# Regrouping the stages of the block chains that lead from the second layer's last product into the third layer

## The chip, the cores and the metric

The kernel runs on one core of a Trainium2 chip. The metric is device time in microseconds (us). One execution taken by the profiler gives the page and the trace that are read here; the median of five timed runs stands beside it.

## The reference, cut to what matters

A graph network of four layers works on x (4096 nodes, 128 features) and one adjacency matrix adj (4096 x 4096, about 0.2% non-zero, kept dense, float32). Each layer is `x = layernorm(x + layer(x, adj))`:

```python
x = _layernorm(x + _L0_gnn_ref(x, adj, adj, ...))   # signed attention
x = _layernorm(x + _L1_gnn_ref(x, adj, ...))        # Chebyshev, K = 3, two convolutions, elu after each
x = _layernorm(x + _L2_gnn_ref(x, adj, ...))        # attention, 4 heads of 32 features
x = _layernorm(x + _L3_gnn_ref(x, adj, ...))        # mean over neighbours
```

The second layer (`_L1_gnn_ref`) ends with a product of adj with a 4096 x 128 matrix, an elu and the layer norm. The third (`_L2_gnn_ref`) is, for every head: `tau = adj_t * exp(max(0.2 C, C))` with `C = alpha_src + alpha_dst`, a sum `tau_sum` over the sources, and `z = sum(adj_t * tau / tau_sum * h_prime)`, where `h_prime = x @ weight.T`.

## The kernel before, in words

The nodes lie in 8 blocks of 512 (`NB = 8`, `IB = 512`), each of 4 tiles of 128. This text calls the last product of the second layer the *big product*; its eight blocks of targets are the loop over `ib` (line L1118). Each block takes 32 matmuls of a 128 x 128 stationary tile against 512 columns. A float32 matmul is recorded as two instructions, so that a block shows 64 of them; a transposition is recorded once.

Three kinds of work are laced into that loop by hand, in an order that PE, DVE, ACT and POOL keep as it is written (`tc.manual_schedule`); the DMA issues on SP are not part of it.

*Block chains.* When block `ib` of the big product is complete, its chain finishes the layer for these 512 nodes. `block_end(ib)` is a generator; each `yield` ends a stage. Its stages, with names that this text uses:

- **elu** (L749 to L753): DVE adds the product, DVE and ACT make the elu in `oT`. It is written at once at the block's end. L749 also frees bank `pp`, in which the next block of the big product accumulates.
- **T1** (L757): four transpositions of `oT` on PE into `px`.
- **N** (L759 to L769): DVE adds to x and takes the statistics, ACT the root, DVE the reciprocal, ACT four activations that normalise x.
- **T2** (L771): four transpositions of x into `px`.
- **C** (L773 to L775): ACT copies to `xT` and loads the table of Exp, POOL adds a bias to x.
- **H0, h0, H1, h1**: H (L784) is two products with `W2S` into `px`, one for each half of the block; h (L791 to L795) reads them, ACT with two exponentials and DVE with two multiplications into `hc`.

`block_targets(ib)` follows with **D** (L804, a product into `px`), **E** (L806, L807: ACT, an exponential and a copy) and **S** (L809 to L813: the split of the result in three bfloat16 parts, which goes DVE, ACT, ACT, DVE, ACT). The last of S on ACT is the last reader of `px`. The pool `ps_x` has one buffer, one PSUM bank: T1, T2, H0, H1 and D of all blocks go through the one `px`, and each waits until the one before it has been read.

*The queue.* The chains stand in one deque, `chains`, and `one(chains)` takes one stage of the first of them; where a generator ends within a call, the call goes on to the next chain. In blocks 3 to 7 of the big product it is called twice in each group of `cuts`: after the group's first half and at its end. With one chunk in a group that is after every 2 matmuls, with two chunks after every 4. A *slot* m is the call after matmul m of the 32. Block 3 has the slots 4, 8, 12, ... 32; blocks 4 and 5 have 2, 4, 6, 8, 12, 16, 18, 20, 22, 24, 28, 32; blocks 6 and 7 have 4, 8, 12, 16, 18, 20, 22, 24, 28, 32.

*Steps of the third layer.* In blocks 3 to 7 each group also carries one source tile `nt` of the third layer for two passes, p0 and p1 (two pairs of heads for the first 1024 targets). ACT copies the tile of adj into the one PSUM buffer `a` (L852); for p0 and then p1 DVE makes `tau` (L880, twice) and a part of `tau2` (L886), and POOL the rest of `tau2` (L887, L888). Every group ends with four products on PE, `num` and `den` (L904, 8 recorded instructions each). The order of a group is: copy `a`, step p0, first half of the matmuls, slot, step p1, second half, slot, four products. Tile `nt` may be started only when the chain of the block that holds it has passed its last stage (`ended`).

The stages of `block_end` are parted by yields such as these, and the halves of H by this loop:

```python
yield
if ib <= 2:
    yield
...
if ib < NB - 2:
    yield
for half in range(2):
```

Of the kernel before, what the change touches and what calls it, by code (L numbers as in the profile page):

```python
# [33 lines left out]
def adj_resnorm_d4(ctx: ExitStack, tc: tile.TileContext, x_in, xT_in, adj, adjT, w0g, w0gT, a0, w1a, b1a,  # L34
# [10 lines left out]
    NB = N // IB  # L45
# [87 lines left out]
    def transpose4(pool, name, src, order=lambda r: r):  # L133

        p = pool.tile([P, TB, P], F32, name=name)
        for k in range(TB):
            order(nc.tensor.transpose(p[:, k, :], src(k), ident))  # L137
        return p

    def stats(r, t):  # L140
        st = small.tile([P, 6], F32, name="st")
        nc.vector.bn_stats(st, r)
        nc.vector.bn_aggr(mv[:, t, :], st)
# [481 lines left out]
    def network(usual):  # L625

        with ExitStack() as whole:
# [113 lines left out]
            def block_end(ib, p):  # L741

                blk = slice(ib * IB, (ib + 1) * IB)
                tb = slice(ib * TB, (ib + 1) * TB)
                pns = []
                oT = l2w.tile([P, IB], F32, name="oT", tag="z")
                rn = l2w.tile([P, 2, IB], F32, name="rn", tag="nd")
                r, n = rn[:, 0, :], rn[:, 1, :]
                nc.vector.tensor_add(oT, p, h0T[:, blk])  # L749
                nc.vector.tensor_scalar(n, oT, B1B, 0.0, op0=ALU.add, op1=ALU.min)  # L750
                nc.scalar.activation(n, n, AF.Exp)
                nc.scalar.activation(r, oT, AF.Relu, bias=B1B)
                nc.vector.scalar_tensor_tensor(oT, n, -1.0, r, op0=ALU.add, op1=ALU.add)  # L753
                yield
                if ib <= 2:
                    yield
                q = transpose4(ps_x, "px", lambda k: oT[:, k * P:(k + 1) * P])  # L757
                yield
                nc.vector.tensor_add(x[:, tb, :], q, x[:, tb, :])  # L759
                for t in range(ib * TB, (ib + 1) * TB):  # L760
                    stats(x[:, t, :], t)
                s = small.tile([P, TB], F32, name="rstd")
                m = small.tile([P, TB], F32, name="mean")
                nc.scalar.activation(s, mv[:, tb, 1], AF.Sqrt, bias=eps)
                nc.vector.reciprocal(s, s)
                nc.vector.scalar_tensor_tensor(m, mv[:, tb, 0], -1.0, s, op0=ALU.mult, op1=ALU.mult)
                for k in range(TB):
                    r = x[:, ib * TB + k, :]
                    nc.scalar.activation(r, r, AF.Identity, bias=m[:, k:k + 1], scale=s[:, k:k + 1])  # L769
                yield  # L770
                q = transpose4(ps_x, "px", lambda k: x[:, ib * TB + k, :])  # L771
                yield
                nc.scalar.copy(xT[:, blk], q.rearrange("p k i -> p (k i)"))  # L773
                nc.scalar.activation(m[:, 0:1], m[:, 0:1], AF.Exp, scale=0.0)
                nc.gpsimd.tensor_tensor(x[:, tb, :], x[:, tb, :], B2R[:, None, :].to_broadcast([P, TB, F]), ALU.add)  # L775
                if ib < NB - 2:
                    yield
                for half in range(2):

                    pool, name = (ps_p, "pp") if ib == NB - 1 and half else (ps_x, "px")  # L780
                    pn = pool.tile([P, 2, F + H], F32, name=name)
                    for k in range(2):
                        t = ib * TB + 2 * half + k
                        nc.tensor.matmul(pn[:, k, :], xT[:, t * P:(t + 1) * P], W2S, start=True, stop=True)  # L784
                    pns.append(pn)
                    if ib == NB - 1 and half == 0:
                        continue
                    yield
                    for pn, at in zip(pns, range(half + 1 - len(pns), half + 1)):
                        two = slice(ib * TB + 2 * at, ib * TB + 2 * at + 2)  # L790
                        nc.scalar.activation(cs[:, two, :], pn[:, :, F:F + H], AF.Exp, scale=0.2)  # L791
                        nc.scalar.activation(es[:, two, :], pn[:, :, F:F + H], AF.Exp, scale=0.8)
                        for k in range(2):
                            t = ib * TB + 2 * at + k
                            nc.vector.tensor_mul(hc[:, t], pn[:, k, 0:F].rearrange("p (h f) -> p h f", f=FO),  # L795
                                                 cs[:, t, :][:, :, None].to_broadcast([P, H, FO]))
                    pns.clear()
                ended.append(ib)

            def block_targets(ib):  # L800

                blk = slice(ib * IB, (ib + 1) * IB)
                pd = ps_x.tile([96, IB], F32, name="px")
                nc.tensor.matmul(pd, WD, xT[:, blk], start=True, stop=True)  # L804
                yield
                nc.scalar.activation(pd, pd, AF.Exp, scale=-0.8)  # L806
                nc.scalar.copy(dv[:, blk], pd)  # L807
                yield
                nc.vector.tensor_sub(pd, pd, dv[:, blk])  # L809
                nc.scalar.copy(dv[32:64, blk], pd[32:64, :])  # L810
                nc.scalar.copy(dv[64:96, blk], pd[64:96, :])
                nc.vector.tensor_sub(pd[64:96, :], pd[64:96, :], dv[64:96, blk])
                nc.scalar.copy(dv[64:96, blk], pd[64:96, :])  # L813
                if ib < 2:
                    yield
# [220 lines left out]
            with tc.manual_schedule(engines={mybir.EngineType.PE, mybir.EngineType.DVE, mybir.EngineType.Activation,  # L1036
# [40 lines left out]
                def num(this, nt, tau2):  # L1077
                    this.product(False, nt, tau2)
                    if nt == NT - 1 and this is not passes[-1]:
                        if this is passes[0]:  # L1080
                            first_sums.close()
                            ps_a.append(enter(name="ps_a2", bufs=1, space=PSUM))
                        chains.append(this.finish())
                        if this.heads[-1] == H - 1:
                            chains.append(layer3_blocks(this.blocks))
                            chains.append(start_product(this.blocks))
                            if this is passes[1]:
                                chains.append(block_targets(NB - 1))
                        later = passes.index(this) + 2
                        if 2 < later < len(passes):  # L1090
                            chains.append(passes[later].targets())
# [13 lines left out]
                for ib in range(NB):  # L1105
                    early = ib == 1
                    p = ps_nd.tile([P, IB], F32, name="num") if early else ps_p.tile([P, IB], F32, name="pp")
                    cuts = [0, 2, 4, 6, 8] if ib < 4 else [0, 1, 2, 4, 5, 6, 8] if ib < 6 else [0, 2, 4, 5, 6, 8]
                    for first, last in zip(cuts, cuts[1:]):
                        ks = [(c, k) for c in range(first, last) for k in range(TB)]  # L1110
                        for n, (c, k) in enumerate(ks):
                            if ib > 2 and n in (0, len(ks) // 2):
                                if n == 0:
                                    load()
                                step()
                            if k == 0:
                                a = chunk(ld, adjT, ib, c)
                            nc.tensor.matmul(p, w[:, c * TB + k, :], a[:, k, :], start=c == 0 and k == 0,  # L1118
                                             stop=c == NB - 1 and k == TB - 1)
                            if n + 1 in (len(ks) // 2, len(ks)) or ib <= 2 and k % 2:  # L1120
                                one(chains)
                        if last == NB:
                            end = block_end(ib, p)
                            next(end)
                            chains.append(end)
                            if ib < NB - 1:
                                chains.append(block_targets(ib))
                            if ib < 2:
                                chains += [this.targets(range(ib, 4, 2)) for this in passes[0:2]]
                        if ib > 2:  # L1130
                            products()
# [79 lines left out]
```

## Time and profile before

| what | value |
|---|---|
| median of 5 runs | 2223.66 us (2220.61 to 2225.76) |
| the profiled execution, its own time | 2222.86 us |
| its span in the trace | 2221.0 us |
| PE busy | 2134.7 us, 96% of the span |
| DVE busy | 1186.5 us, 53% |
| POOL busy | 857.7 us, 39% |
| ACT busy | 562.8 us, 25% |
| DMA | 528.18 MB, mean 238 GB/s |

The span is the time between the first and the last recorded instruction; 1.86 us of the execution's own time lie outside it. The blocks of the big product can be told in the trace by L749, which starts as each block's last matmul is done: it starts at 1169.55 us for block 2, 1211.39 for block 3, 1272.49 for block 4, 1329.81 for block 5, 1380.51 for block 6 and 1430.55 for block 7. "In block 4" below means the stretch in which the big product's block 4 runs, which is when the chain of block 3 is worked off.

### The profile page before, as it was taken

Reading aid. Unit: us, or ns where it says so; the run is one execution under the profiler, and the core shown is the slowest. Engines: PE = TensorE matmul, PEld = TensorE weight load, DVE = VectorE, ACT = ScalarE, POOL = GpSimd, SP = SyncE. Lnnn points to the kernel's source line nnn. Section 1 sums busy time; section 2 is a strip of 40 time slices with the busy share of each in tenths; the row PEclk is TensorE's granted clock in tenths of the full one; section 3 lists DMA queues with packets and bytes.
Section 4 is the critical chain, followed back from the end, with each engine's and each line's share of the span. In section 5 each row is a group of like instructions: output and inputs, shape, how many; then the busy total and the mean of one; then the engine's idle time right before and its main releaser. Section 6 shows DMA issues by size and latency. Waiting matters only on the chain. (4 is left out here: it accounts for less than half of the span.)

```text
span 2221.0 us, 22997 instructions
## 1 busy us (share of the span) xinstructions
PE 2134.7 (96%) x8640; PEld 847.9 (38%) x8644; DVE 1186.5 (53%) x1832; ACT 562.8 (25%) x1014; POOL 857.7 (39%) x539
## 2 busy tenths in 40 slices
PE   8999999999999999999999999979999899999997
PEld 3444454444444444444443333322222222223333
DVE  5655560000011110000017777799999999999995
ACT  6755010000000000000032323335333433232213
POOL 0000000000000000000005676698999899989980
PEclk9999999999999999999999999999999999999999
DMA  9886658888767667777876556525666566635554
GB/s 395 337 326 234 223 192 290 300 301 303 265 229 260 240 233 269 263 264 264 292 256 232 189 195 218 209 82 193 240 231 241 190 244 230 228 133 191 189 174 170
DMA packets 87145, 528.18 MB, mean 238 GB/s; under 512 B 9328, under 2 KB 15472, under 8 KB 25712
## 3 DMA queue, kind: packets, MB, share of 16 engines
q1 hardware_dynamic: 80288, 521.64, 66.8%
q10 hardware_dynamic: 6736, 4.98, 0.7%
q8 instruction: 70, 1.15, 0.2%
q14 instruction: 51, 0.42, 0.1%
HBM read 524.49 MB, written 2.10 MB: 237 GB/s over the span
## 5 line engine op out<-in xcount | busy, mean ns | idle before, releaser
L880 DVE SCALAR_TENSOR_TENSOR tau<-D,es,a 128x1024 f32<-128x1024 f32 (+1 forms) x640 | 646.7, 1059 | 45.9 <-ACT a L852 20.0
L888 POOL TENSOR_TENSOR tau<-tau,chunk 128x1024 f32<-128x1024 f32 x192 | 459.6, 2394 | 13.3 <-DVE tau L880 12.7
L775 POOL TENSOR_TENSOR x<-x,B2R 128x512 f32<-128x512 f32 x8 | 10.2, 1276 | 1143.8 <-PE px L137 1143.8
L904 PE MATMUL num<-tau,hc 128*32 128x512 f32 x2048 | 331.6, 614 | 15.6 <-POOL tau L888 9.1
L904 PE MATMUL den<-tau,cs 128*32 128x512 f32 x2048 | 337.5, 603 | 1.8 <-DVE tau L880 0.4
L991 PE MATMUL pp<-chunk,xT 128*128 128x512 f32 (+1 forms) x488 | 231.7, 604 | 0.0
L852 ACT ACTIVATE a<-chunk 128x1024 f32<-128x1024 f32 x160 | 164.4, 1027 | 248.7 <-DVE tau L886 188.1
L664 PE MATMUL pacc<-chunk,t 128*128 128x512 f32 x512 | 223.5, 592 | 0.0
L664 PE MATMUL pacc<-chunk,v 128*128 128x512 f32 x512 | 222.5, 592 | 0.0
L664 PE MATMUL pacc<-chunk,x 128*128 128x512 f32 x512 | 222.1, 592 | 0.0
L887 POOL TENSOR_TENSOR tau<-tau,chunk 128x320 f32<-128x320 f32 x192 | 168.2, 876 | 128.0 <-DVE tau L880 85.3
L1118 PE MATMUL pp<-chunk,w 128*128 128x512 f32 x448 | 203.1, 598 | 0.8 <-DVE oT L749 0.8
L379 PE MATMUL pacc<-chunk,hw 128*128 128x512 f32 x408 | 188.2, 606 | 0.8 <-DVE hw L421 0.7
L886 DVE TENSOR_TENSOR tau<-tau,a 128x704 f32<-128x704 f32 x186 | 163.4, 878 | 0.0
L894 POOL TENSOR_TENSOR tau<-tau,chunk 128x1024 f32<-128x1024 f32 x64 | 151.7, 2371 | 1.1
L904 PEld LDWEIGHTS num<-tau,hc 128*32 128x32 f32 x2048 | 61.3, 110 | 229.8 <-issue 129.2
L904 PEld LDWEIGHTS den<-tau,cs 128*32 128x32 f32 x2048 | 79.0, 111 | 174.6 <-issue 99.0
L664 PEld LDWEIGHTS pacc<-chunk,v 128*128 128x128 f32 x512 | 97.2, 190 | 122.0 <-issue 122.0
L664 PEld LDWEIGHTS pacc<-chunk,x 128*128 128x128 f32 x512 | 96.3, 190 | 115.8 <-issue 115.8
L664 PEld LDWEIGHTS pacc<-chunk,t 128*128 128x128 f32 x512 | 96.1, 190 | 115.3 <-issue 115.3
L991 PEld LDWEIGHTS pp<-chunk,xT 128*128 128x128 f32 x488 | 85.7, 189 | 128.6 <-issue 125.8
L711 DVE COPY w<-ptr 128x512 f32<-128x512 f32 x8 | 5.5, 692 | 241.5 <-PE ptr L137 241.5
(243 smaller groups left out, 1687.8 us busy)
## 6 DMA issues: line engine op xcount, KB each, us to landing
chunk<-in_adjT SPq DMA_DIRECT2D x386, 1024.0 KB, 4.8
chunk<-in_adj SPq DMA_DIRECT2D x80, 1024.0 KB, 4.9
chunk<-in_adj SPq DMA_DIRECT2D x32, 512.0 KB, 4.7
keep<-in_adjT SPq DMA_DIRECT2D x13, 1024.0 KB, 9.9
xT<-in_xT ACTq DMA_DIRECT2D x8, 256.0 KB, 6.7
out<-o ACTq DMA_DIRECT2D x7, 256.0 KB, 2.3
W1A<-in_w1a ACTq DMA_DIRECT2D x1, 384.0 KB, 5.6
W1B<-in_w1b ACTq DMA_DIRECT2D x1, 384.0 KB, 7.6
```

The lines of the kernel that those rows point to most:

```text
L379: in_order(nc.tensor.matmul(p, hw[:, j * TB + k, :], a[:, k, :], start=first and k == 0, stop=last and k == TB - 1))
L664: nc.tensor.matmul(p, stationary(c * TB + k), a[:, k, :], start=n == 0 and k == 0, stop=n == NB - 1 and k == TB - 1)
L775: nc.gpsimd.tensor_tensor(x[:, tb, :], x[:, tb, :], B2R[:, None, :].to_broadcast([P, TB, F]), ALU.add)
L852: nc.scalar.activation(ap, a, AF.Copy, accum_out=deg[:, nt, self.mp:self.mp + 1])
L880: nc.vector.scalar_tensor_tensor(flat(tau[:, q:q + n]), flat(self.D[:, q:q + n]), es[:, nt, head:head + 1], ap, op0=ALU.max, op1=ALU.mult)
L886: nc.vector.tensor_tensor(t2[:, 0:OWN], t[:, 0:OWN], (a if only else ap)[:, 0:OWN], ALU.mult)
L887: nc.gpsimd.tensor_tensor(t2[:, OWN:WB], t[:, OWN:WB], a[:, OWN:WB], ALU.mult)
L888: nc.gpsimd.tensor_tensor(t2[:, WB:2 * WB], t[:, WB:2 * WB], a, ALU.mult)
L894: nc.gpsimd.tensor_tensor(tau2[:, 2:4, :], tau[:, 2:4, :], rep(a, 2), ALU.mult)
L904: nc.tensor.matmul(acc[32 * q:32 * q + 32, :], weights(nt, head, is_den), r[:, q, :], start=nt == 0, stop=nt == NT - 1)
L991: nc.tensor.matmul(p, y[:, c * TB + k, :], a[:, k, lo:lo + n], start=c == blocks[0] and k == 0, stop=end)
L1118: nc.tensor.matmul(p, w[:, c * TB + k, :], a[:, k, :], start=c == 0 and k == 0, stop=c == NB - 1 and k == TB - 1)
```

## The change

Four yields move. In `block_end`, block 2 loses the empty stage ahead of T1 (blocks 0 and 1 keep it) and the yield between C and H0. Blocks 3 and 4 get a yield ahead of H1, so that h0 and H1 are no longer taken in one call. In `block_targets`, blocks 3 to 6 get a yield ahead of D, so that h1 and D are no longer taken in one call. No instruction is added or taken away; the places of the stages among the matmuls and steps change.

```diff
-                if ib <= 2:
+                if ib < 2:
                     yield
                 q = transpose4(ps_x, "px", lambda k: oT[:, k * P:(k + 1) * P])
...
-                if ib < NB - 2:
+                if ib < NB - 2 and ib != 2:
                     yield
                 for half in range(2):
 
                     pool, name = (ps_p, "pp") if ib == NB - 1 and half else (ps_x, "px")
+                    if half and ib in (3, 4):
+                        yield
                     pn = pool.tile([P, 2, F + H], F32, name=name)
...
             def block_targets(ib):
 
                 blk = slice(ib * IB, (ib + 1) * IB)
+                if 2 < ib < NB - 1:
+                    yield
                 pd = ps_x.tile([96, IB], F32, name="px")
```

## The prediction

> **What bounds the kernel now.** I read the page's busy shares first, then PE's list of waits over blocks 3 to 7 of the big product (1168 to 1431 us), a table of busy times by block, and the timeline where the longest wait lies.
>
> ```profile
> ## 1 busy us (share of the span) xinstructions
> PE 2134.7 (96%) x8640; PEld 847.9 (38%) x8644; DVE 1186.5 (53%) x1832; ACT 562.8 (25%) x1014; POOL 857.7 (39%) x539
> ```
>
> PE has the work. A change that only moves stages can win what PE waits, no more. The waits:
>
> ```profile
> PE px L137 <- ACT dv L813: 5.4, 1, 5.4
> PE px L784 <- DVE hc L795: 1.8, 2, 1.5
> PE px L804 <- DVE hc L795: 0.9, 1, 0.9
> PE pp L1118 <- DVE oT L749: 0.8, 1, 0.8
> PE px L137 <- ACT x L769: 0.6, 1, 0.6
> PE num L904 <- POOL tau L888: 0.6, 1, 0.6
> ```
>
> Total, times, longest. Three of the six, 8.1 us, are px products that wait for px's last reader. By block (stretch, its length, busy PE, PEld, DVE, ACT and POOL with instruction counts, clock granted to PE, DMA share, GB/s):
>
> ```profile
> 1169.55:1211.39 41.84, 40.86 (x169) 16.81 (x170) 31.05 (x42) 11.41 (x23) 26.93 (x17) 1.00 0.67 226
> 1211.39:1272.49 61.10, 55.71 (x280) 20.21 (x282) 46.74 (x58) 19.34 (x37) 39.67 (x25) 0.94 0.52 189
> 1272.49:1329.81 57.32, 55.59 (x278) 19.51 (x281) 45.34 (x57) 16.58 (x32) 38.26 (x26) 1.00 0.55 202
> ```
>
> Blocks 4 and 5 hold the same work, yet block 4 is 3.8 us longer, at a clock of 0.94. The reason in PE's timeline:
>
> ```profile
> 1215.71 3.70 PE L1118 MATMUL pp<-chunk,w 128*128 128x512 f32 x8
> 1224.80 1.11 PE L137 MATMUL px<-ident,oT 128*128 128x128 f32 x4 [5.39 <-ACT dv L813]
> 1225.84 1.94 PE L904 MATMUL num<-tau,hc 128*32 128x512 f32 x8
> 1227.55 1.69 PE L904 MATMUL den<-tau,cs 128*32 128x512 f32 x8
> 1229.07 1.03 PE L904 MATMUL num<-tau,hc 128*32 128x512 f32 x8
> ```
>
> T1 of block 3 waits for S of block 2, written in the same slot 4. S stands on DVE behind both steps of nt 4 (they end at 1221.5) and takes 2.6 us there. Then two groups of eight run at 1.71 and 1.52 us instead of 0.86.
>
> **What the Trainium skill says.** "PSUM — Partial Sum Buffer", section "Engine vs sequencer instructions": the queues of ScalarE, VectorE and GpSimd are strictly first in, first out, and matmuls start in program order. The trace agrees: S waits on DVE behind steps that it doesn't need. "TensorE: Matmul & The Clock Gate", section "What's actually happening": after an idle window of about 3.4 us PE runs at half rate until it has been busy for about as long, and the window is free-running. The trace agrees: slow after 5.39 us, not after the 1.52 us at 1361.09. "ScalarE: Activation LUTs", section "What ACT_TABLE_LOAD costs": 1283 ns for a load. The trace has 1.28 us; it lies ahead of N's root while ACT waits for the statistics, before and after.
>
> **The slots, counted from the code.** Before, chain 2 in block 3: T1 8, N 12, T2 16, C 20, H0 24, h0+H1 28, h1+D 32; E, S+T1 in slots 2, 4 of block 4. After: T1 4, N 8, T2 12, C+H0 16, h0+H1 20, h1+D 24, E 28, S 32. Chain 3 in block 4, before: N 6, T2 8, C 12, H0 16, h0+H1 18, h1+D 20. After: T1 2, N 4, T2 6, C 8, H0 12, h0 16, H1 18, h1 20, D 22, E 24, S 28. Up to H0 that is how chain 4 already lies in block 5. Below, times are against before; minus is earlier.
>
> **Block 3: +0.33.** T1 comes at about 1173.9, oT is ready at 1172.76: no wait. N now follows p1 of nt 0 on DVE (1179.5). In block 5 (before) N begins at 1282.49, ACT normalises from 1285.68, and the copy a for the next tile stands behind that:
>
> ```profile
> 1286.22 1.48 PE L137 MATMUL px<-ident,x 128*128 128x128 f32 x4 [0.64 <-ACT x L769]
> 1288.46 2.47 DVE L880 SCALAR_TENSOR_TENSOR tau<-D,es,a 128x1024 f32<-128x1024 f32 x2 [2.82 <-ACT a L852]
> ```
>
> So DVE begins nt 1 at 1179.5+6.0=1185.5 instead of 1180.78. PE reaches T2 at 1184.04, its last operand comes at 1184.4: 0.15 lost, where before T2 lost 0.97 (1187.60 to 1189.12, less 0.55). The products of nt 1 just hold: num needs POOL at step start+4.92=1190.4 and comes at 1190.5. C+H0: xT is ready at 1186.1, PE comes at 1188.3. At slot 20 PE comes at 1195.75, but h0 stands on DVE behind p0 of nt 2: nt 1 takes two steps of 3.19 to 1191.9, copy 1.27, step 3.19, h0 0.5: 1196.9. H1 waits 1.15. D: h1 ends 1200.6, PE comes 1201.0. Sum -0.97+0.15+1.15. H1's wait is not in the trace of before; bounds 0 and 2.1 (nothing, or nt 1 a further us late), taken 1.15. S goes into DVE's idle ahead of L749 (2.67 us); px is free at about 1212, T1 comes at 1217.9, so the 5.39 us wait goes. What is late next is T2.
>
> **Block 4: -3.40.** The old stall: T1 could start at 1219.25 and PE goes on with L1118 at 1230.89, 11.64 us for what takes 4.10 at 1234.42 to 1238.52: 7.54 lost. The new placement costs what it costs in block 5: there the second group takes 11.69 (1283.60 to 1295.29) against 7.64 of the first (1275.96 to 1283.60), 4.05 lost in T2 and in products that wait for DVE and POOL, which are late by N. PE's lead over L749 is 3.39 there instead of 3.47: 0.08 more. -7.54+4.05+0.08=-3.41, the same as 22.81 (1215.71 to 1238.52) becoming 19.41. Bounds of the 4.05: 0 (N hidden) and 5.5 (the copy a late once more). H1 and D waited for nothing here before (four matmuls or a step lay between), so their new slots give 0. DVE's tail fits: by the same rows it is ready for L749 about 1 us before PE.
>
> **Block 5: -0.33.** T2 and the products are tied to L749 again (third group at L749+22.8), which moves by 3.0, not 3.07. H1 in its own slot saves 0.32 of wait and 0.08 of slow start.
>
> **Block 6: -0.59.** H1 waits 1.52 for h0, a chain of DVE and ACT from L749 on: 31.14 us here, 30.55 in block 5, since L750 took 1.08 instead of 0.49 while POOL worked. After, POOL is through before L750. Bounds 0 and -0.59; I take the second. S of block 5 now stands in front of L749 in slot 32: DVE is free at about 1379.8 before, PE needs L749's end at 1383.98: 2.8 us of cover; gone, each us of lateness costs one.
>
> **Block 7: -0.93.** D waits 0.88 for h1, and starts slowly; two matmuls and four products now lie between. No slot runs out: chain 6 ends in slot 28.
>
> After block 7 the order is as before, so the rest shifts whole. SP's loads keep their order, and PE shows no wait for a load. POOL gets one bias addition (1.28 us) earlier, in a gap.
>
> Sum: 0.33-3.40-0.33-0.59-0.93=**-4.9 us**. The execution's own time 2222.86 (span 2221.0 and 1.86 outside) becomes 2217.9; the median stands 0.8 above it, so 2218.8.
>
> **Rivals.** *DVE pays it back* (0.17): N ahead of the copy a costs block 3 the 4.05 that it costs block 5, not 1.3: -4.9+2.75=-2.2, or 2221.5. For it: products that hold by 0.1 us; against it: block 3 has 4 matmuls, 3.4 us, more for each tile. *The clock* (0.10), on the other side: the short waits at T2 and H1 in block 3, at T2 and at the products in block 4 each tip PE into half rate, at the 2.0 us that the stall at 1219 cost in slow running: -4.9+8=+3.1, or 2226.8. It decides where an almost idle stretch fills the window; block 5 has two such waits at a clock of 1.00, which speaks against it. *The change doesn't free T1* (0.07): elu's oT (1215.9) comes over 2 us late behind S, and T1 waits for that: -3, or 2220.7.
>
> **The numbers.** The main case has 0.66 and runs from -9 (N hidden in block 4) to -1.5 (block 3 at its bound, block 6 and 7 without gain). The range 2214.5 to 2223.5 takes in the first and third rival and leaves out the clock. The line is 0.2%, 4.4 us, about what a measurement of this kernel can tell from no change. Faster: 0.56 of the main case and 0.04 of the rivals; within: 0.10 and 0.20; slower: the clock's 0.10.
>
> **What would show it.** Right: no wait of px for L813; block 4's clock near 1.00, its length near 57 us; a wait of T2 for L769 in block 4; H1 in block 3 waiting about 1 us for hc; none for D in block 7. Wrong: groups of eight at 1.5 us or more in blocks 3 or 4, pp waiting for L749 at the start of blocks 4 or 7, or DVE idle over 3 us ahead of L880 in more places than once a block.

## The result, and the profile after

The kernel after takes 2217.78 us (median of 21 runs, 2215.95 to 2222.63), the kernel before 2223.51 us beside it (41 runs). The ratio is 0.9977 with a 95% interval of 0.9971 to 0.9983: 5.1 us less, between 3.8 and 6.4. The profiled execution took 2217.91 us, with a span of 2216.1 us against 2221.0.

In the new code the lines below the moved yields have other numbers: L1118 is L1122, L904 is L908, L784 is L786, L804 is L808, L813 is L817, L880 is L884, L852 is L856, L888 is L892. L749 to L775 keep theirs.

The page's busy shares of the kernel after:

```profile
## 1 busy us (share of the span) xinstructions
PE 2134.3 (96%) x8640; PEld 847.4 (38%) x8644; DVE 1186.4 (54%) x1832; ACT 562.9 (25%) x1014; POOL 857.6 (39%) x539
```

No engine has less to do. What changed is what PE waits for. Its waits in the kernel after, from 1168 to 1431 us (total, times, longest):

```profile
PE px L786 <- DVE hc L797: 2.1, 2, 1.1
PE px L137 <- ACT x L769: 1.4, 2, 0.8
PE num L908 <- POOL tau L892: 1.2, 2, 0.6
PE pp L1122 <- DVE oT L749: 0.8, 1, 0.8
PE px L137 <- DVE oT L753: 0.7, 1, 0.7
```

The wait for the last reader of `px` (5.4 us for L813) is gone, and so is D's (0.9 for hc). T2 of chain 3 now waits in block 4 as T2 of chain 4 did in block 5, and the last line is new: T1 of block 7 waits for elu. By block, in the windows of the kernel after (stretch, its length, busy PE, PEld, DVE, ACT and POOL with counts, clock, DMA share, GB/s):

```profile
1170.24:1213.27 43.03, 41.27 (x174) 16.77 (x178) 32.37 (x45) 14.07 (x28) 26.88 (x17) 1.00 0.61 217
1213.27:1270.04 56.77, 55.35 (x278) 19.43 (x280) 45.36 (x57) 16.60 (x32) 38.64 (x25) 1.00 0.56 206
1270.04:1326.93 56.89, 55.34 (x278) 19.42 (x280) 45.48 (x56) 16.60 (x32) 39.77 (x26) 1.00 0.57 203
```

Block 4 is now as long as block 5, and its clock is 1.00 instead of 0.94. PE's timeline where the long stall was (start, length, and in brackets the idle time before it):

```profile
1216.73 1.98 PE L1122 MATMUL pp<-chunk,w 128*128 128x512 f32 x4
1218.55 0.60 PE L137 MATMUL px<-ident,oT 128*128 128x128 f32 x4
...
1220.80 1.07 PE L908 MATMUL num<-tau,hc 128*32 128x512 f32 x8
...
1227.01 1.48 PE L137 MATMUL px<-ident,x 128*128 128x128 f32 x4 [0.65 <-ACT x L769]
...
1231.02 1.81 PE L908 MATMUL den<-tau,cs 128*32 128x512 f32 x8
```

T1 stands in slot 2 and waits for nothing; the next group of eight runs at its full rate. What is late next is T2, and behind it the products of that group: a group of eight is stretched to 1.81 us, and PE waits 0.60 us more ahead of one of the last `num` (1234.23). The clock granted to this block is 1.00, so this group is long because it waits for its operands.

### The profile page after: what moved, and what is told of

The parts are those of the page before. It is cut to its first block, busy times and chain, and to the rows that moved or that the text cites. A ratio compares the mean times of both kernels' runs of the same rounds, so it can differ in the third digit from the quotient of the medians.

```text
span 2216.1 us, 22992 instructions
## 1 busy us (share of the span) xinstructions
PE 2134.3 (96%) x8640; PEld 847.4 (38%) x8644; DVE 1186.4 (54%) x1832; ACT 562.9 (25%) x1014; POOL 857.6 (39%) x539
## 3 DMA queue, kind: packets, MB, share of 16 engines
q8 instruction: 70, 1.15, 0.2%
## 5 line engine op out<-in xcount | busy, mean ns | idle before, releaser
L884 DVE SCALAR_TENSOR_TENSOR tau<-D,es,a 128x1024 f32<-128x1024 f32 (+1 forms) x640 | 646.6, 1059 | 46.4 <-ACT a L856 24.0
L892 POOL TENSOR_TENSOR tau<-tau,chunk 128x1024 f32<-128x1024 f32 x192 | 459.7, 2394 | 12.3 <-DVE tau L884 11.6
L775 POOL TENSOR_TENSOR x<-x,B2R 128x512 f32<-128x512 f32 x8 | 10.2, 1276 | 1144.5 <-PE px L137 1144.5
L908 PE MATMUL num<-tau,hc 128*32 128x512 f32 x2048 | 333.2, 611 | 16.3 <-POOL tau L892 9.6
L908 PE MATMUL den<-tau,cs 128*32 128x512 f32 x2048 | 338.7, 601 | 2.0 <-DVE tau L884 0.4
L856 ACT ACTIVATE a<-chunk 128x1024 f32<-128x1024 f32 x160 | 164.4, 1027 | 253.6 <-DVE tau L890 193.2
L1122 PE MATMUL pp<-chunk,w 128*128 128x512 f32 x448 | 204.3, 598 | 0.8 <-DVE oT L749 0.8
L908 PEld LDWEIGHTS num<-tau,hc 128*32 128x32 f32 x2048 | 61.7, 110 | 237.5 <-issue 130.6
L908 PEld LDWEIGHTS den<-tau,cs 128*32 128x32 f32 x2048 | 79.2, 111 | 173.4 <-issue 97.9
```

Source lines behind the costliest of these rows:

```text
L856: nc.scalar.activation(ap, a, AF.Copy, accum_out=deg[:, nt, self.mp:self.mp + 1])
L884: nc.vector.scalar_tensor_tensor(flat(tau[:, q:q + n]), flat(self.D[:, q:q + n]), es[:, nt, head:head + 1], ap, op0=ALU.max, op1=ALU.mult)
L892: nc.gpsimd.tensor_tensor(t2[:, WB:2 * WB], t[:, WB:2 * WB], a, ALU.mult)
L908: nc.tensor.matmul(acc[32 * q:32 * q + 32, :], weights(nt, head, is_den), r[:, q, :], start=nt == 0, stop=nt == NT - 1)
```

## The experiments

Each was timed in turn with the kernel before on the same chip. "Blocks 3 to 7" is the time from L749 of block 2 to L749 of block 7 in each kernel's profile. Block times repeat within 0.05 us where the order is the same (block 6 of the kernel after: 50.25 and 50.26 in two profiles). From T2 of block 7 to the end every kernel has the same work; this stretch took 774.0 to 777.6 us in the profiles. It falls into two groups by PE's clock: where the clock granted between 1940 and 1980 us is 0.96 (after, e2, e4, e6, e7, e9, e10) it took 774.0 to 775.2 us, where it is 0.91 (before, e1, e3, e5, e8, e11) 776.1 to 777.6. This spread is about as large as the effects studied here, so the blocks show an effect more sharply than the total does.

| kernel | block 3 | 4 | 5 | 6 | 7 | blocks 3 to 7 | ratio to before, 95% interval |
|---|---|---|---|---|---|---|---|
| before | 41.84 | 61.10 | 57.32 | 50.70 | 50.04 | 261.00 | |
| after | 43.03 | 56.77 | 56.89 | 50.25 | 49.11 | 256.05 | 0.9977 (0.9971 to 0.9983) |
| e1: only block 2's yields | 43.04 | 57.32 | 57.93 | 50.72 | 50.04 | 259.05 | 0.9985 (0.9979 to 0.9992) |
| e2: only the later blocks' | 41.84 | 61.61 | 56.76 | 50.28 | 48.94 | 259.43 | 0.9990 (0.9981 to 0.9998) |
| e6: block 2 one stage less | 42.78 | 59.59 | 56.89 | 50.23 | 48.95 | 258.44 | 0.9990 (0.9982 to 0.9998) |
| e8: after without D's yield | 43.04 | 57.36 | 57.37 | 50.11 | 50.03 | 257.91 | 0.9982 (0.9975 to 0.9988) |
| e4: before, T1 a slot later | 41.85 | 62.76 | 57.31 | 50.73 | 50.04 | 262.69 | 1.0002 (0.9995 to 1.0008) |
| e9: before, the stall filled | 41.84 | 60.45 | 57.32 | 50.73 | 50.03 | 260.37 | 0.9994 (0.9987 to 1.0) |
| e3: after, N apart | 43.03 | 59.36 | 58.69 | 50.12 | 48.94 | 260.14 | 1.0002 (0.9993 to 1.0010) |
| e5: after, N and T2 apart | 43.02 | 55.52 | 55.51 | 50.11 | 48.94 | 253.10 | 0.9966 (0.9953 to 0.9979) |

### The two halves of the change

Block 2's two yields alone (e1_block2_only):

```diff
-                if ib <= 2:
+                if ib < 2:
...
-                if ib < NB - 2:
+                if ib < NB - 2 and ib != 2:
```

> Only the two yields of block 2 are taken away; the yields ahead of H1 and D are not added. If the stall of block 3's T1 behind S of block 2 is what counts: no wait of px for ACT's last copy of S, block 4 near 57 us like block 5, H1 of blocks 4 and 5 waiting 0.3 us each for hc, D of block 7 still waiting 0.9: about -3.5 us against before. If the later yields carry the gain: within 1 us of before.

The later blocks' yields alone (e2_later_only):

```diff
+                    if half and ib in (3, 4):
+                        yield
...
+                if 2 < ib < NB - 1:
+                    yield
```

> Only the yields ahead of H1 (blocks 3 and 4) and D (blocks 3 to 6) are added; block 2 keeps its stages. Theory of the stall: T1 still waits some 5.4 us in block 4, and only the waits at H1 in block 5 and D in block 7 go, part of which DVE pays back at the end of block 7: -0.5 us, between 0 and -1.5. If the later yields carry the gain: -3 us or more.

Block 2's yields alone gave 3.3 us (1.8 to 4.7) in the runs and 1.95 in the blocks: block 4 lost 3.78, block 3 grew by 1.20, block 5 by 0.61. The later yields alone gave 2.2 us (0.4 to 4.2), 1.6 of it in the blocks, a little more than the bound of what I expected. The stall is gone in e1 and unchanged in e2, as PE's list of waits of e2 shows:

```profile
PE px L137 <- ACT dv L817: 5.4, 1, 5.4
```

So block 2's yields free T1, as the prediction says. The halves are worth more together (4.95 in the blocks) than apart (1.95 and 1.57). In e1, once block 4 has no stall, H1 there waits 0.32 us in the call that also holds h0, and T2 in block 5 waits 1.25 us instead of 0.64, as L750 takes 1.09 there (the last section tells why). Behind that wait PE ran four instructions at half speed, 3.46 us instead of 1.88, which the last section shows too.

Only one of block 2's two yields removed (e6_one_stage), against the kernel after:

```diff
-                if ib < NB - 2 and ib != 2:
+                if ib < NB - 2:
```

> The changed kernel, but block 2 gives up only the stage ahead of T1 and keeps the yield between C and H0. S of block 2 then falls into slot 2 of block 4, again in one call with T1 of block 3. Theory of the shared slot: T1 waits some 5 us for ACT's last copy of S, the matmuls after it run slow, and little of the gain is left: 0 to -2 us against before. If each stage taken off block 2 brings its share: about -3.

It gave 2.2 us (0.4 to 4.0) in the runs and 2.6 in the blocks, between the two outcomes that I had named. With one stage less, S and T1 come in one slot again, slot 2 instead of 4: T1 waits 4.81 us for L817. Taking one stage off block 2 brings 1.0 us in the blocks (e6 beside e2, which has the same later yields and keeps both of block 2's); the second brings the other 2.4. To lose the wait itself, the last stage of one chain must be over before the next chain's T1 is written.

The yields ahead of D taken away (e8_no_d_slot), against the kernel after:

```diff
-                if 2 < ib < NB - 1:
-                    yield
```

> The changed kernel without the yields ahead of D: block 2's two yields away, H1 of blocks 3 and 4 in its own slot. Theory: D follows h1 at once and waits 0.8 to 0.9 us in blocks 4, 5 and 7; the last of them cost the changed kernel's DVE about as much at the end of block 7: +1 to +2.5 us against the changed kernel, -2.5 to -4 against before. If D's own slot brings nothing: the same as the changed kernel.

The blocks took 1.86 us more than in the kernel after: 0.59 in block 4, 0.48 in block 5, 0.92 in block 7, and 0.14 less in block 6. D waits 0.40, 0.40 and 0.87 us for hc in blocks 4, 5 and 7, in the first two half of what I expected. In the kernel before D waits in block 7 alone, and so it does in e1, which has no stall but takes h0 and H1 in one call: there H1 waits 0.32 and 0.31 us in blocks 4 and 5, just ahead of D. So D waits in these blocks once H1 has a slot of its own and PE no longer loses that time at H1; the yields ahead of H1 and of D belong together.

### What the stall was worth

The kernel before with one empty stage more ahead of T1 of block 3 (e4_t1_apart):

```diff
-                if ib <= 2:
+                if ib <= 3:
```

> The kernel before with one yield more ahead of T1 in block 3's chain alone (slot 6 instead of 4), so that S of block 2 and T1 no longer share a slot; N falls into slot 8. Theory: the 5.4 us wait and the slow matmuls go (7.5 us), N ahead of the copy costs 4 us, H1 and D come at slots that follow h at once and wait about 1 us each: -1.6 us, between 0 and -3. If the wait is DVE's lateness rather than the shared slot, T1 waits nearly as long in slot 6: 0 or slower.

No gain: ratio 1.0002 (0.9995 to 1.0008), and 1.7 us more in the blocks. I expected a gain of 1.6. T1 no longer waits, and at first this pays: the third group of block 4 starts 21.39 us after L749 of block 3, where it starts after 27.13 in the kernel before and after 22.80 in the kernel after. But every later stage of chain 3 comes a slot later, and H1, in the same call as h0, waits 3.74 us. In PE's timeline of e4:

```profile
1233.94 3.70 PE L1118 MATMUL pp<-chunk,w 128*128 128x512 f32 x8
...
1254.19 0.69 PE L784 MATMUL px<-W2S,xT 128*128 128x132 f32 x4 [3.74 <-DVE hc L795]
1254.81 1.84 PE L904 MATMUL num<-tau,hc 128*32 128x512 f32 x8
1256.40 1.95 PE L904 MATMUL den<-tau,cs 128*32 128x512 f32 x8
```

The reason is where DVE takes h0, in its timelines of the kernel before and of e4:

```profile
1247.67 0.48 DVE L795 TENSOR_TENSOR hc<-px,cs 128x128 f32<-128x128 f32 x2
```

```profile
1253.56 0.48 DVE L795 TENSOR_TENSOR hc<-px,cs 128x128 f32<-128x128 f32 x2
```

In the kernel before h0 is written in the middle of a group (slot 18), and DVE takes it between the steps p0 and p1, while PE has four products behind H0 (1245.49) and two matmuls. In e4 h0 is a slot later and stands behind both steps (1247.19 to 1253.6), and PE has only two matmuls behind H0 (1248.12) before it needs `px` again. So a stall of this size came back at H1, the third product behind T1 that writes `px`; T2 and H0 between them wait for nothing. It brought its slow groups with it (1.84 and 1.95 us instead of some 1.05). A slot of its own for T1 wins the stall, then, if no later stage pays for it; the change gives T1 that slot by ending chain 2 earlier, so that chain 3 need not come later. Whether S has to leave block 4 is not shown: no run keeps S there with T1 apart and h0 and H1 well placed.

To see what the slow groups alone are worth, the stall of the kernel before was filled with six products of a zero tile, added to the same bank (e7_busy_stall, then e9_busy_stall_late). They change no value.

```diff
+                            if ib == 4 and first == 0 and n + 1 == len(ks):
+                                for _ in range(6):
+                                    nc.tensor.matmul(p, zero, a[:, k, :], start=False, stop=False)
```

> The kernel before with 6 matmuls of a zero tile (12 recorded instructions of 0.43 us, 5.2 us) added to the big product's bank in block 4 just ahead of S and T1 of slot 4, so that PE is busy while T1 waits. If the slow matmuls after the stall come from PE's idleness: T1 starts as before, the groups after it run in 0.86 us, block 4 is 2.0 us shorter, -2 us against before. If they come from something else: 0, or up to +5 if T1 did not wait for DVE and ACT.

> The same 6 zero matmuls ahead of T1 in block 4 of the kernel before, but the zero tile is set by POOL just ahead of the big product and not at the start of the kernel, where it moved the first layer's start by some 5 us. Theory from the trace of the first try: T1 starts as before, the eight-groups after it take 0.86 us, but T2 then waits for N, so that block 4 is 0.7 us shorter, not 2.0: -0.7 us against before. If PE's slow running is a loss of its own: -2.0.

e7 was 3.3 us slower (1.0015, 1.0008 to 1.0021). Its zero tile was written by DVE at the kernel's start, and the first layer came later: L749 of block 2 starts at 1174.23 us, in all other profiles between 1169.55 and 1171.72. So its total doesn't answer the question. In its blocks it won 0.68. In e9 POOL writes the tile just ahead of the big product: 0.63 us less in the blocks, 0.9994 (0.9987 to 1.0) in the runs. PE's timeline of e9:

```profile
1219.66 5.31 PE L1124 MATMUL pp<-chunk,zero 128*128 128x512 f32 x12
1225.21 0.66 PE L137 MATMUL px<-ident,oT 128*128 128x128 f32 x4 [0.24 <-ACT dv L813]
1225.80 1.07 PE L904 MATMUL num<-tau,hc 128*32 128x512 f32 x8
1226.68 1.04 PE L904 MATMUL den<-tau,cs 128*32 128x512 f32 x8
...
1233.30 1.48 PE L137 MATMUL px<-ident,x 128*128 128x128 f32 x4 [0.23 <-ACT x L769]
```

T1 comes no sooner, but nothing behind it is slow: the groups start 0.86 to 0.88 us apart, where the kernel before has 1.71 and 1.52. So the slow clock comes from the idle time, as the Trainium skill says in "TensorE: Matmul & The Clock Gate", section "What's actually happening". Its 2.0 us were worth only 0.65 of block 4, since T2 then waits for N instead: it starts 0.23 us late and takes 1.48 us, where the kernel before has no wait and 0.60.

### What is left: N ahead of the copy

In the kernel after DVE still sits idle in block 4 for the copy of the next tile, which stands on ACT behind the normalising of x. In DVE's timeline of the kernel after (x2: two instructions):

```profile
1229.25 2.47 DVE L884 SCALAR_TENSOR_TENSOR tau<-D,es,a 128x1024 f32<-128x1024 f32 x2 [2.83 <-ACT a L856]
```

One stage more, an empty one, between T1 and N for blocks 3 and 4 puts N behind p0 of the next tile, after that tile's copy (e3_n_apart):

```diff
                 q = transpose4(ps_x, "px", lambda k: oT[:, k * P:(k + 1) * P])
...
+                if ib in (3, 4):
+                    yield
```

> The changed kernel, and for the chains of blocks 3 and 4 one more yield between T1 and N, so that N falls into slot 6, in the first half of the second group, and the copy a of the next tile no longer stands behind it on ACT. If N ahead of the copy is what blocks 4 and 5 still lose: the 2.8 us of DVE idle and the waits of T2 and of the products go there, each block 2.8 to 4.0 us shorter (53 to 54 us), -5.6 to -8 against the changed kernel, -10.5 to -13 against before. If DVE's work as such bounds these blocks, or S, which now falls into the last slot ahead of L749, holds up the next block: under 1 us each.

A plain miss: 1.0002 (0.9993 to 1.0010), and 4.1 us more in the blocks than the kernel after. The 2.83 us of DVE are gone, but T2 stands in the next slot, with two matmuls and no products of the third layer between. PE's timeline of e3:

```profile
1232.80 1.64 PE L137 MATMUL px<-ident,x 128*128 128x128 f32 x4 [3.47 <-ACT x L771]
1234.37 1.94 PE L910 MATMUL num<-tau,hc 128*32 128x512 f32 x8
```

T2's wait for its own operand x grew from 0.65 to 3.47 us, in block 5 too, and PE's clock fell to half behind it (0.94 granted in block 4, 0.97 in block 5). I had costed N's place on DVE and forgotten the product behind it.

With an empty stage between N and T2 too, and C and H0 taken together in blocks 3 and 4 so that the chain still ends in time (e5_n_t2_apart; e11_n_t2_again is the same kernel on another chip):

```diff
+                if ib in (3, 4):
+                    yield
...
+                if ib in (3, 4):
+                    yield
...
-                if ib < NB - 2 and ib != 2:
+                if ib < NB - 2 and ib not in (2, 3, 4):
```

> The changed kernel with, for the chains of blocks 3 and 4, a yield between T1 and N and one between N and T2, and C taken together with H0: T1 2, N 6, T2 12, C+H0 16, h0 18, H1 20, h1 22, D 24, E 28, S 32. Theory: with N off the path of the copy a and T2 two slots behind N, PE waits neither at T2 nor at the products of the second group; DVE, which then has 55.5 us of work per block, sets the pace of blocks 4 and 5 instead of 56.8: -2.6 us against the changed kernel, between 0 and -4, so -6 to -9 against before. If blocks 4 and 5 are held by DVE's work alone: within 1 us of the changed kernel.

> The version with N in slot 6 and T2 in slot 12 for the chains of blocks 3 and 4, beside the changed kernel on one chip: blocks 2 to 7 take 253.1 us again, 2.9 less than the changed kernel; -2.9 us against it, -8 against before. If its first lead was chance: no more than 1 us.

> The changed kernel once more, beside the next one: blocks 2 to 7 take 256.0 us from L749 to L749 as in its first profile, the whole -5 us against before. If the stretch after block 7 is set by the kernel, it takes 775.2 us from T2 of block 7 to the end again; if by the phase of PE's clock, another value between 774.0 and 777.5.

This one beats the kernel before: 0.9966 (0.9953 to 0.9979) and, beside a second set of runs of the kernel after (e10_after_again: 2217.78 us, 0.9975, 0.9967 to 0.9983), 2216.12 us, 0.9964 (0.9952 to 0.9976). Against the kernel after the medians differ by 1.7 us, and the intervals of e10 and e11 overlap, so the runs alone don't show that lead. The blocks do: 253.10 and 253.14 us against 256.05 and 256.09, 2.95 less each time. Part of it is not in the totals of the profiles, as the stretch behind T2 of block 7 took 776.1 and 777.2 us in e5 and e11, 775.2 and 774.7 in the two profiles of the kernel after. That this stretch moved by 0.5 us between two profiles of one kernel also answers in part what e10 asked: the kernel alone doesn't set it. The larger steps go with the two groups of the clock; what moved the 0.5 us stays open. PE's waits in e5:

```profile
PE den L912 <- DVE tau L888: 2.8, 2, 1.4
PE px L790 <- DVE hc L801: 1.9, 2, 1.0
```

T2 is no longer among them. A product of each of blocks 4 and 5 waits 1.4 us for a step of DVE, so it seems to be DVE's steps that pace these blocks now. At the end of block 4, DVE waits only 0.32 us for the big product ahead of L749.

## Why the prediction was right, and where a step failed

Its steps can be held against places that the trace has. Shifts against the kernel before, both counted from L749 of block 2 (which starts 0.69 us later in the profile after, before anything of the change has run):

| place | predicted | measured |
|---|---|---|
| first L1118 (L1122) after block 3's end: 1215.71, 1216.73 | +0.33 | +0.33 |
| third group of block 4: 1238.52, 1236.07 | -3.07 | -3.14 |
| L749 of block 5: 1329.81, 1326.93 | -3.40 | -3.57 |
| L749 of block 6: 1380.51, 1377.18 | -3.99 | -4.02 |
| L749 of block 7: 1430.55, 1426.29 | -4.92 | -4.95 |
| T2 of block 7 | -4.92 | -4.14 |

- **Block 3.** H1's wait measured 1.01 us for 1.15, T2 waits for nothing. The block is 1.19 us longer from L749 to L749, but 0.86 of that is D itself, which stood behind L749 in slot 32 before and stands ahead of it in slot 24 now. PE's own work came 0.33 later, as in the sum.
- **Block 4.** The row borrowed from block 5 held: T2 waits 0.65, DVE 2.83 ahead of L884, the third group starts 22.80 after L749 (predicted 22.8). That H1 and D wait for nothing there was true only behind the stall: e1 has H1 waiting 0.32 us and e8 D 0.40. The change's yields kept it true.
- **Block 5.** From the third group of block 4 to L749 of block 5 0.43 was gained, 0.10 more than predicted.
- **Block 6.** 0.45 was gained instead of 0.59: H1's wait went from 1.52 to 1.06, since L750 there takes 0.62 us instead of 1.08. "After, POOL is through before L750" did not hold: POOL ended at 1327.99, 0.33 us after L750 had started.
- **Block 7.** D's 0.93 came in full: e8, without the yield, has 50.03, the kernel after 49.11.

What the prediction named as signs of being right all came. One sign of being wrong came too, a group of eight of over 1.5 us in block 4 (1.81), but with the clock at 1.00: it waited for DVE and POOL, which the sum had counted.

**The step that failed** is "After block 7 the order is as before, so the rest shifts whole". By then PE had gained so much that DVE had no idle time left ahead of L749 of block 7, and POOL was still at work. DVE's timeline of the kernel after:

```profile
1425.49 0.88 DVE L890 TENSOR_TENSOR tau<-tau,a 128x704 f32<-128x704 f32 x1
1426.29 0.68 DVE L749 TENSOR_TENSOR oT<-pp,xT 128x512 f32<-128x512 f32 x1
1427.01 1.31 DVE L750 TENSOR_SCALAR rn<-oT,B1B 128x512 f32<-128x512 f32 x1
1429.63 0.69 DVE L753 SCALAR_TENSOR_TENSOR oT<-rn 128x512 f32<-128x512 f32 x1 [1.31 <-ACT rn L752]
```

and POOL's beside it:

```profile
1425.65 2.39 POOL L892 TENSOR_TENSOR tau<-tau,chunk 128x1024 f32<-128x1024 f32 x1 [0.26 <-DVE tau L884]
```

In the kernel before, POOL's instruction was nearly over when L750 of block 7 started (it ended at 1431.39), and DVE's timeline there has:

```profile
1431.28 0.49 DVE L750 TENSOR_SCALAR rn<-oT,B1B 128x512 f32<-128x512 f32 x1
```

L750 takes 1.31 us instead of 0.49, L753 is late by that, and T1 waits for it:

```profile
1430.37 0.66 PE L137 MATMUL px<-ident,oT 128*128 128x128 f32 x4 [0.71 <-DVE oT L753]
```

0.8 of the 4.95 us is paid back there. I had seen the same lengthening in block 6 of the kernel before and counted its end as a gain; I did not ask where the new timing would bring it about. That the profiled span still fell by 4.9 us, as predicted, is partly luck: 4.1 us less up to T2 of block 7, 1.4 less behind it, and 0.7 more ahead of L749 of block 2. The stretch behind varies by 3.5 us over kernels whose work there is the same, so its 1.4 us are no effect that I can tie to the change. The runs (3.8 to 6.4 us less) hold both 4.1 and 4.9.

**The rivals.** *DVE pays it back*: block 3's products hold, PE comes at +0.33 and not +3.1; DVE took 0.8 back at block 7, by another way. *The clock*: blocks 3 and 4 wait 1.01 us at H1 and 0.65 at T2 and keep a clock of 1.00. The mechanism is real, at 3.47 us in e3 and 3.74 in e4, and it was not far off: in e1 it set in behind a wait of 1.25 us at T2. *T1 not freed*: `oT` was ready at 1216.48, and T1 started at 1218.55 without a wait.

## What to carry to other kernels

A stall on a buffer with one copy can be won by parting the late reader from the product that waits for it, but everything behind that product moves too. Here it paid to end the earlier chain sooner; pushing the later chain back by a slot won the stall at T1 and lost it again at H1 (e4). When a stage moves, place its producer and its consumer with it: the slots between them must hold enough PE work to cover the producer (e4 at h0 and H1, e3 at N and T2). And when PE catches up on the vector engines, go on to the next block boundary with the new times, and see which work on DVE and POOL now overlaps that did not before.

## What the runs showed of the hardware

L750, a TENSOR_SCALAR of 128x512 from SBUF to SBUF, takes 0.49 us alone. Where POOL's L892 (L888) is at work as it starts, and has more than 0.2 us to go, L750 ends 0.27 to 0.29 us after POOL does: in the kernel after at 1428.32, POOL at 1428.04; in the kernel before at 1331.61, POOL at 1331.34; in e1 at 1272.97, POOL at 1272.68; in e2 at 1432.99, POOL at 1432.71. Its length follows what POOL has left: 0.62 us where POOL ends 0.33 us after its start (block 5 of the kernel after), 1.31 us where that is 1.03 (block 7), and still 0.49 us where it is 0.18 or 0.11 (kernel before, at 1381.24 and 1431.28). So POOL's instruction sets the end of L750. Why it does is argued: the Trainium skill, "SBUF — State Buffer", section "Who interferes with whom", says that a tensor_scalar can take the port pair that DVE shares with GpSimd, and that the one that issues second is blocked until the first has finished. The trace agrees in that L750, which starts second, always ends after POOL. L750 ends 0.28 us after POOL and not 0.49, though, so some 0.2 us of it (an estimate from these two) ran while POOL still worked. No run changed the ports that either instruction uses.

For PE's clock, take all profiles from L749 of block 2 to T2 of block 7. Every wait of 3.26 us or more went with a stretch at half clock: 3.47 (e3, twice), 3.74 (e4), 4.81 (e6), 5.39 us (before and e2), and the 3.26 or 3.27 us that T2 of block 7 waits in each of them (a clock of 0.86 from 1435 to 1460 us). The cost differed: two groups of eight at 1.5 to 1.7 us apiece behind the 5.39 us of the kernel before, but only one T1 and four matmul instructions slowed, at 1.11 and 2.87 us, behind the 4.81. Waits of up to 1.54 us did not bring it, with one exception, T2 of block 5 in e1:

```profile
1285.49 1.63 PE L137 MATMUL px<-ident,x 128*128 128x128 f32 x4 [1.25 <-ACT x L769]
1286.91 3.46 PE L1118 MATMUL pp<-chunk,w 128*128 128x512 f32 x4
```

The clock granted to that block is 0.97. The prediction took from the Trainium skill that it needs an idle window of about 3.4 us; the waits of 1.25 and 3.26 us were shorter than that, so the length of one wait does not decide alone. What PE must do within a window to keep its clock is not shown by these runs.
